# Four graph layers on one core: order of the prologue's loads and masks, and the feed-forward norms' engines

## The chip, the cores and the metric

The kernel runs on one core of a Trainium2 chip. A core has five engines that each work through their own list of instructions in order: TensorE (PE in the profile, with its weight loads as PEld), VectorE (DVE), ScalarE (ACT), GpSimd (POOL) and SyncE (SP), which here only issues loads and stores (DMAs). Engines wait for one another by semaphores. The metric is the device time of one execution in microseconds, taken as a median over runs; a separate execution is profiled, and all times of single instructions come from that one.

## The reference

For 16 batches of 1024 nodes with 256 features and one adjacency matrix, four layers follow one another, each with a residual:

```
h = relu(layernorm(x));  x = x + layer_L(h, adj)
layer 0, 1:  h = x @ W;  e = leaky_relu(h.a1[:, None] + h.a2[None, :])   # 1 head
             softmax over edges (adj != 0 in layer 0, adj > 0 in layer 1) @ h;  relu (0) or elu (1)
layer 2:     8 heads of dot-product attention, masked by adj > 0;  t
             x1 = layernorm(x + t) * ln1_g + ln1_b
             f  = relu(x1 @ w1 + b1) @ w2 + b2
             layernorm(x1 + f) * ln2_g + ln2_b
layer 3:     as layer 1 with 4 heads of 64, elu
```

In the inputs the biases are zero and the gains one, but the kernel computes with them as given.

## The kernel before

All lines are those of the profile. The function `fast_path` holds the whole work; `general_path` runs only if a check at the end fails, and did not run. The kernel writes out the order of instructions by hand: what the program emits first on an engine runs first there.

**Prologue (L314 to L400).** `load_x(0)` loads the first batch in one DMA on SP's queue (L317). `gat_weights` (L334) loads a layer's weights (L340) and its two attention vectors (L344), spread to all 128 partitions, on ACT's queue, and forms the products W.a1 and W.a2 on VectorE (L349), which become three more columns per head of the weights `wx`. Layer 0's come first. Then, for each of eight row blocks, the adjacency is loaded (L364), compared with zero in two ways (L367: `mask_nz` for layer 0, `mask_pos` for the others; the same instruction counts the degree), transposed by TensorE (L370, eight transposes) and copied by ScalarE into a byte mask (L371). Then come the loads of batches 1 and 2, layer 1's weights, the weights of layer 2 with gains and offsets (`spread`, L331) and layer 3's weights, whose eight vectors share three buffers with their products.

**Main loop.** The work of a layer and batch is a `Stage`. Its way in (`way_in`) is, for each of eight row blocks: statistics (`stats_of`: L501, L503 on VectorE, then the reciprocal root on GpSimd, L505 and L506), the normalized rows, transposes (L518, copied out at L519), the projection (L523), and in the layers 0, 1 and 3 the exponentials and scaled values (L563 to L572). Then weights and aggregation: in layers 0 and 1 `gat_front` spreads the source terms (L624, L629) and makes weights (L634), and `gat_back` multiplies (L647); in layer 2 `dot_front` makes scores (L811), exponentials (L817) and masks them (L822), and `dot_back` multiplies (L833); in layer 3 `pair_front` makes weights (L707) and `pair_back` multiplies (L727, L738).

Aggregation is cut into slots. After each slot `side_work` emits what is due of a queue: pieces put there by `later` or `chain` with a delay, and with a guess of their PE and DVE time, of which a slot takes at most 1.8 to 3.0 us each. `settle` empties the queue as far as needed when the next stage must be ready. Batches go in pairs: layers 0 and 1 of a pair, then layer 2 of both, then layer 3 mixed with layers 0 and 1 of the next pair.

**Feed-forward norms.** After the attention of half a batch, `feed_forward` takes four row blocks through `stats`, `norm`, `turn` (transposes into TensorE's layout and adds b2 to the rows on GpSimd, L898), two matrix products and a second norm (`finish`). `norm` calls `affine` (L511 to L513), which uses three engines in turn:

```
nc.scalar.activation(y, y, AF.Identity, scale=-1.0, bias=m)          # m - y
nc.vector.scalar_tensor_tensor(y, y, r, g, ALU.mult, ALU.mult)       # (m - y) r g
nc.gpsimd.tensor_tensor(y, b, y, ALU.subtract)                       # b - that
```

**Layer 3's elu** (`pair_out`): GpSimd takes one from x (L781) while ScalarE forms exp(y) (L785); VectorE then adds max(y, 0) (L788) and min(exp(y), 1) (L789).

Of the kernel before, what the change touches and what calls it, by code (L numbers as in the profile page):

```python
# [37 lines left out]
P = 128  # L38
# [13 lines left out]
def flat(a):  # L52
    return a.rearrange("f o -> (f o)")


def one_row(v):
    return v.rearrange("(o f) -> o f", o=1)
# [230 lines left out]
def fast_path(tc, bad, x, adj, l0_w, l0_a, l1_w, l1_a, w_qkv, ln1_g, ln1_b, ln2_g, ln2_b, w1, b1, w2, b2, l3_w, l3_a, out):  # L288
# [13 lines left out]
    with ctx:  # L302
# [12 lines left out]
        def load_x(b):  # L315
            xs[b] = state.tile([P, NT, C], F32, tag="x", name=f"x{b}", bufs=3)
            nc.sync.dma_start(out=xs[b], in_=x[b].rearrange("(t p) c -> p t c", p=P))  # L317
# [6 lines left out]
        ident_b = work.tile([P, P], BF16, tag="o", name="ident_b", bufs=2)  # L324
# [4 lines left out]
        def spread(v, name):  # L329
            t = const.tile([P, v.shape[0]], F32, name=name)  # L330
            nc.scalar.dma_start(out=t, in_=one_row(v).to_broadcast([P, v.shape[0]]))  # L331
            return t

        def gat_weights(w_heads, a1s, a2s, alpha, name):  # L334
# [4 lines left out]
            for h in range(heads):  # L339
                nc.scalar.dma_start(out=wx[:, :, h * hs : (h + 1) * hs], in_=rows(w_heads[h]))  # L340
            for h in range(heads):
                for a, uses in ((a1s[h], ((0, alpha - 1.0),)), (a2s[h], ((1, 1.0 - alpha), (2, alpha)))):
                    ab = work.tile([P, hs], F32, tag="xn", name="ab", bufs=3)
                    nc.scalar.dma_start(out=ab, in_=one_row(a).to_broadcast([P, hs]))  # L344
                    for part, factor in uses:
                        for k in range(KC):
                            col = C + part * heads + h
                            scr = work.tile([P, hs], F32, tag="xn", name="scr", bufs=3)
                            nc.vector.scalar_tensor_tensor(  # L349
                                scr, wx[:, k, h * hs : (h + 1) * hs], factor, ab, ALU.mult, ALU.mult,  # L350
                                accum_out=wx[:, k, col : col + 1],
                            )
            return wx

        wx0 = gat_weights([l0_w], [flat(l0_a[:C])], [flat(l0_a[C:])], ALPHA[0], "l0")
# [6 lines left out]
        for t in range(NT):  # L362
            edges = work.tile([P, N], I32, tag="p", name="edges", bufs=9)
            nc.sync.dma_start(out=edges, in_=adj[t * P : (t + 1) * P, :])  # L364
            for which, (op, mask) in enumerate(((ALU.not_equal, mask_nz), (ALU.is_gt, mask_pos))):
                m = work.tile([P, N], BF16, tag="p", name="m", bufs=9)
                nc.vector.tensor_scalar(m, edges, 0.0, 0.0, op, ALU.add, accum_out=degree[:, which, t : t + 1])  # L367
                tp = ps_mm.tile([P, NT, P], BF16, tag="mm", name="tp_mask")
                for j in range(NT):
                    nc.tensor.transpose(tp[:, j, :], m[:, j * P : (j + 1) * P], ident_b)  # L370
                nc.scalar.copy(mask[:, :, t * P : (t + 1) * P], tp)  # L371

        load_x(1)
        load_x(2)

        wx1 = gat_weights([l1_w], [flat(l1_a[:C])], [flat(l1_a[C:])], ALPHA[1], "l1")
        qkv_sb = const.tile([P, KC, 3 * C], F32, name="qkv_sb")
        nc.scalar.dma_start(out=qkv_sb, in_=rows(w_qkv))
        w1_sb = const.tile([P, KC, C], F32, name="w1_sb")
        nc.scalar.dma_start(out=w1_sb, in_=rows(w1))  # L380
        w2_sb = const.tile([P, KC, C], F32, name="w2_sb")
        nc.scalar.dma_start(out=w2_sb, in_=rows(w2))
        b1_sb = const.tile([P, KC, 1], F32, name="b1_sb")
        nc.scalar.dma_start(out=b1_sb, in_=b1.rearrange("(k p o) -> p k o", p=P, o=1))
        g1_sb, be1_sb = spread(ln1_g, "g1_sb"), spread(ln1_b, "be1_sb")
        g2_sb, be2_sb = spread(ln2_g, "g2_sb"), spread(ln2_b, "be2_sb")
        b2_sb = spread(b2, "b2_sb")
        wx3 = gat_weights(
            [l3_w[h] for h in range(H3)], [l3_a[h, :HS3] for h in range(H3)],
            [l3_a[h, HS3:] for h in range(H3)], ALPHA[3], "l3",  # L390
        )
        WX = {0: wx0, 1: wx1, 2: qkv_sb[:, :, 2 * C :], 3: wx3}
# [116 lines left out]
        def affine(y, m, r, g, b):  # L509

            nc.scalar.activation(y, y, AF.Identity, scale=-1.0, bias=m)  # L511
            nc.vector.scalar_tensor_tensor(y, y, r, g, ALU.mult, ALU.mult)  # L512
            nc.gpsimd.tensor_tensor(y, b, y, ALU.subtract)  # L513
# [237 lines left out]
        def pair_out(s, hp):  # L751
# [15 lines left out]
            for n in range(NH):  # L767
# [5 lines left out]
                def turn(n=n, y3=y3, xo=xo):  # L773
# [7 lines left out]
                    nc.gpsimd.tensor_scalar(xo, xo, -1.0, None, ALU.add)  # L781


                def power(ex=ex, y3=y3):
                    nc.scalar.activation(ex, y3, AF.Exp)  # L785

                def leave(n=n, ts=ts, ex=ex, y3=y3, xo=xo):
                    nc.vector.scalar_tensor_tensor(xo, y3, 0.0, xo, ALU.max, ALU.add)  # L788
                    nc.vector.scalar_tensor_tensor(xo, ex, 1.0, xo, ALU.min, ALU.add)  # L789
# [91 lines left out]
        def feed_forward(s, n):  # L881
            T_of = {"turned": 0}
            for i in range(TH):
# [10 lines left out]
                def turn(yt=yt, i=i):  # L894
# [3 lines left out]
                    nc.gpsimd.tensor_add(yt, yt, b2_sb)  # L898

                def turned(turn=turn):  # L900
# [6 lines left out]
                    (2.0, stats, 0.0, 0.6, None), (3.0, norm, 0.0, 0.5, None),  # L907
# [15 lines left out]
            def finish(t, i):  # L923
# [18 lines left out]
                chain((2.5, second, 0.9, 1.0, None), (3.0, norm, 0.0, 0.5, None))  # L942
# [58 lines left out]
        for t in range(NT):  # L1001
            way_in(by_key[0, 0], t, 1.0 * t)
        settle(by_key[0, 0])
        for s, piece in early:
            piece()

# [84 lines left out]
```

## Time and profile before

| | us |
|---|---|
| median of 3 runs | 4930.01 (4928.68 to 4932.11) |
| the profiled execution | 4923.55 |
| its span, first to last instruction | 4921.7 |
| mean granted TensorE clock | 0.980 |
| first layer norm starts | 78.31 |
| first aggregation on TensorE starts | 102.54 |
| one pair of batches, start to start | 601 |

The profile names a group by line, engine, operation and what it writes and reads; then come busy time, the mean of one in ns, and the idle time of the engine just before such instructions with what ended it. A stretch's row gives its length, the busy time of each engine and the granted TensorE clock. The clock is 1.00 for most of the run and drops to half for some us at a time; a stretch's number is the mean. A busy PE is not a PE at its peak.

### The profile page before, as it was taken

Reading aid. Unit: us, or ns where it says so; the run is one execution under the profiler, and the core shown is the slowest. Engines: PE = TensorE matmul, PEld = TensorE weight load, DVE = VectorE, ACT = ScalarE, POOL = GpSimd, SP = SyncE. Lnnn points to the kernel's source line nnn. Section 1 sums busy time; section 2 is a strip of 40 time slices with the busy share of each in tenths; the row PEclk is TensorE's granted clock in tenths of the full one; section 3 lists DMA queues with packets and bytes.
Section 4 is the critical chain, followed back from the end, with each engine's and each line's share of the span. In section 5 each row is a group of like instructions: output and inputs, shape, how many; then the busy total and the mean of one; then the engine's idle time right before and its main releaser. Section 6 shows DMA issues by size and latency. Waiting matters only on the chain.

```text
span 4921.7 us, 61508 instructions
## 1 busy us (share of the span) xinstructions
PE 4572.1 (93%) x22546; PEld 2264.1 (46%) x22546; DVE 3522.8 (72%) x5992; ACT 2219.7 (45%) x4017; POOL 1990.7 (40%) x2424
## 2 busy tenths in 40 slices
PE   4999899998999989999899998999999999999997
PEld 3843357433573335733357334562346623565232
DVE  4558876688756877578775788757877588775787
ACT  2356532564335642366323663236633466334651
POOL 1315642155422553225532356313653145531453
PEclk9999999999999999999999999999999999999999
DMA  2000010000100000000010000100010000100001
GB/s 89 1 1 1 18 35 18 1 1 18 35 18 1 1 18 35 18 1 18 1 46 7 1 18 9 44 1 1 18 34 19 1 1 18 35 9 1 1 18 36
DMA packets 50917, 79.13 MB, mean 16 GB/s; under 512 B 5680, under 2 KB 41136, under 8 KB 50608
## 3 DMA queue, kind: packets, MB, share of 16 engines
q1 hardware_dynamic: 45440, 71.58, 4.3%
q10 hardware_dynamic: 5168, 3.54, 0.3%
q8 instruction: 181, 2.97, 0.2%
q14 instruction: 128, 1.05, 0.1%
HBM read 58.07 MB, written 17.04 MB: 15 GB/s over the span
## 4 chain that ended last, share of the span: by engine, by line
PE 73%; DVE 10%; ACT 6%; POOL 6%; issue 3%; DVEq 0%; DMA 0%; ACTq 0%; POOLq 0%
PE pm L523 17%; PE av L647 17%; PE acc L833 12%; PE sc L811 10%; PE acc L727 8%; PE sums L738 4%; DVE p L707 3%; PE tp L518 3%; DVE pe L822 2%; POOL y L513 2%; ACT pe L817 2%; POOL rstd L506 2%; PE rp L624 1%; DVE y L512 1%; POOL rstd L505 1%
## 5 line engine op out<-in xcount | busy, mean ns | idle before, releaser
L822 DVE TENSOR_TENSOR pe<-pe,mask_pos 128x1024 f32<-128x1024 f32 x1024 | 1304.6, 1320 | 383.8 <-ACT pe L817 383.2
L817 ACT ACTIVATE pe<-sc 128x1024 f32<-128x1024 f32 x1024 | 991.8, 1021 | 448.0 <-PE sc L811 447.9
L833 PE MATMUL acc<-pe,v 128*33 128x512 f32 x4096 | 1010.4, 615 | 21.9 <-DVE pe L822 21.8
L505 POOL TENSOR_SCALAR rstd<-stats 128x1 f32<-128x1 f32 x768 | 398.2, 519 | 1421.8 <-DVE stats L503 1400.9
L647 PE MATMUL av<-v,p 128*128 128x257 f32 x4096 | 946.0, 380 | 0.8 <-DVE p L634 0.7
L647 PEld LDWEIGHTS av<-v,p 128*128 128x128 f32 x4096 | 756.3, 190 | 129.2 <-issue 28.8
L506 POOL TENSOR_TENSOR rstd<-rstd,minus_half 128x1 f32<-128x1 f32 x768 | 655.8, 854 | 64.0
L811 PE MATMUL sc<-qT,kT 32*128 32x512 f32 x4096 | 650.1, 654 | 16.9 <-ACT pe L817 16.9
L707 DVE SCALAR_TENSOR_TENSOR p<-r,e,mask_pos 128x1024 f32<-128x1024 f32 x512 | 654.8, 1324 | 13.8 <-PE sums L738 13.4
L833 PEld LDWEIGHTS acc<-pe,v 128*33 128x33 f32 x4096 | 198.4, 112 | 754.6 <-issue 422.3
L727 PE MATMUL acc<-p,v 128*64 128x512 f32 x2048 | 483.3, 614 | 3.1 <-ACT e L568 3.1
L523 PE MATMUL pm<-l_wx,hT 128*128 128x259 f32 (+1 forms) x1536 | 418.2, 403 | 27.6 <-ACT v L570 19.5
L864 POOL TENSOR_TENSOR y<-y,z 128x256 f32<-128x256 f32 x128 | 97.3, 768 | 794.8 <-DVE z L860 793.7
L523 PEld LDWEIGHTS pm<-l_wx,hT 128*128 128x128 f32 x1536 | 281.2, 194 | 173.4 <-issue 59.7
L519 ACT ACTIVATE hT<-tp 128x256 f32<-128x256 f32 x640 | 239.2, 384 | 265.2 <-PE tp L518 264.1
L811 PEld LDWEIGHTS sc<-qT,kT 32*128 32x128 f32 x4096 | 197.8, 185 | 315.6 <-ACT pe L817 203.4
L513 POOL TENSOR_TENSOR y<-be_sb,y 128x256 f32<-128x256 f32 x256 | 307.7, 1214 | 41.9 <-DVE y L512 41.6
L660 DVE RECIPROCAL inv<-av 128x1 f32<-128x1 f32 x256 | 42.8, 167 | 385.1 <-PE av L647 385.1
L518 PE MATMUL tp<-ident,xn 128*128 128x128 f32 x1024 | 206.3, 291 | 83.9 <-POOL rstd L505 44.1
L727 PEld LDWEIGHTS acc<-p,v 128*64 128x64 f32 x2048 | 138.5, 140 | 310.3 <-issue 246.1
L501 DVE BATCH_NORM_STATS2 st<-x 128x6 f32<-128x256 f32 x512 | 214.0, 418 | 91.3 <-POOL x L665 64.6
L665 POOL TENSOR_TENSOR x<-x,o 128x256 f32<-128x256 f32 x128 | 101.8, 796 | 387.7 <-ACT o L664 383.5
(98 smaller groups left out, 4872.7 us busy)
## 6 DMA issues: line engine op xcount, KB each, us to landing
r<-kept SPq DMA_DIRECT2D x64, 512.0 KB
x<-in_x_dram SPq DMA_DIRECT2D x16, 1024.0 KB
out_dram<-x SPq DMA_DIRECT2D x64, 256.0 KB
edges<-in_adj_dram SPq DMA_DIRECT2D x8, 512.0 KB
kept<-rows_sb SPq DMA_DIRECT2D x128, 2.0 KB
qkv_sb<-in_L_gnn_w_qkv_dram ACTq DMA_DIRECT2D x1, 768.0 KB
l_wx<-in_L_gnn_W_dram ACTq DMA_DIRECT2D x2, 256.0 KB
ab<-in_L_gnn_a_dram ACTq DMA_DIRECT2D x4, 128.0 KB
```

Source lines behind the costliest of these rows:

```text
L505: nc.gpsimd.tensor_scalar(r, stats[:, 1:2], EPS, None, ALU.add)
L506: nc.gpsimd.tensor_tensor(r, r, minus_half, ALU.pow)
L513: nc.gpsimd.tensor_tensor(y, b, y, ALU.subtract)
L518: nc.tensor.transpose(tp[:, k, :], src[:, k * P : (k + 1) * P], ident)
L523: nc.tensor.matmul(dst, lhsT=lhsT[:, k, :], rhs=rhs[:, k, :], start=(k == 0), stop=(k == KC - 1))
L647: nc.tensor.matmul(av[:, : s.hs + 1], lhsT=box[j // 2][:, j % 2, i * P : (i + 1) * P], rhs=s.v[:, j, h, :], start=(j == 0), stop=(j == NT ...
L707: nc.vector.scalar_tensor_tensor(p, s.r[hp][:, hh, :], s.e[:, j, col : col + 1], mask_pos[:, j, :], ALU.max, ALU.mult)
L727: both(lambda jj, n, hh, h, p: nc.tensor.matmul(s.acc[n][hh * hs : (hh + 1) * hs, :], lhsT=s.v[:, jj, h, :hs], rhs=p, start=(jj == 0), sto ...
L811: nc.tensor.matmul(sc[:, hh, :], lhsT=s.kT[r0 : r0 + D2, g, j * P : (j + 1) * P], rhs=s.qT[r0 : r0 + D2, g, cols], start=True, stop=True,)
L817: nc.scalar.activation(p, sc, AF.Exp, scale=SCALE2)
L822: nc.vector.tensor_tensor(box[pair], box[pair], m, ALU.mult)
L833: nc.tensor.matmul(s.acc[pair][hh * 64 : hh * 64 + D2 + 1, :], lhsT=s.v[:, j, h, :], rhs=box[pair][:, hh, :], start=(j == 0), stop=(j == N ...
```

## The change

- The first batch is loaded in halves. All loads but layer 0's weights and vectors go to SP's queue, in this order: batch 0, the eight blocks of adjacency, batch 1, the weights of layers 1 and 3, `qkv`, batch 2, the rest of layer 2's, and as the last two the second bias, once as a row and once as a column. The attention vectors of a layer come in one load of 256 KB. The adjacency stays in four large buffers.
- Layer 0's products come first, then its way in. Its mask is then made in two halves around the first weights. The other products (`fill1`, `fill3`), `fold_bias` and `mask_pos` become side work of the first slots.
- `affine` is two VectorE instructions. The second bias is added into the offset of the first norm, and w1 times it is taken from the first bias, so that L898 goes.
- Layer 3's elu: GpSimd's step goes; ScalarE forms relu(1 - exp(y)) and VectorE subtracts it.
- The guessed DVE time of `norm` is 1.0 in place of 0.5.

```diff
         def load_x(b):
-            nc.sync.dma_start(out=xs[b], in_=x[b].rearrange("(t p) c -> p t c", p=P))
+            for n in range(NH):
+                ts = slice(n * TH, (n + 1) * TH)
+                nc.sync.dma_start(out=xs[b][:, ts, :], in_=x[b, n * HALF : (n + 1) * HALF, :].rearrange("(t p) c -> p t c", p=P))
...
-        def gat_weights(w_heads, a1s, a2s, alpha, name):
+        def gat_weights(eng, w_heads, a, alpha, name):
...
-                    ab = work.tile([P, hs], F32, tag="xn", name="ab", bufs=3)
-                    nc.scalar.dma_start(out=ab, in_=one_row(a).to_broadcast([P, hs]))
+            ab = work.tile([P, 2 * C], F32, tag="p", name="ab", bufs=9)
+            eng.dma_start(out=ab, in_=one_row(a).to_broadcast([P, 2 * C]))
+            def fill(h):
...
+            return wx, [lambda h=h: fill(h) for h in range(heads)]
+        wx0, fill0 = gat_weights(nc.scalar, [l0_w], flat(l0_a), ALPHA[0], "l0")
+        edges = [state.tile([P, 2, N], I32, tag="big", name="edges", bufs=4) for _ in range(NT // 2)]
+        for t in range(NT):
+            nc.sync.dma_start(out=edges[t // 2][:, t % 2, :], in_=adj[t * P : (t + 1) * P, :])
+        load_x(1)
+        wx1, fill1 = gat_weights(nc.sync, [l1_w], flat(l1_a), ALPHA[1], "l1")
...
+        b2_row = work.tile([P, 2 * C], F32, tag="p", name="b2_row", bufs=9)
+        nc.sync.dma_start(out=b2_row[:, :C], in_=one_row(b2).to_broadcast([P, C]))
+        b2_col = const.tile([P, KC, 1], F32, name="b2_col")
+        nc.sync.dma_start(out=b2_col, in_=b2.rearrange("(k p o) -> p k o", p=P, o=1))
+
+        def fold_bias():
+            nc.vector.tensor_add(be1_sb, be1_sb, b2_row[:, :C])
+            for m in range(KC):
+                pm = ps_mm.tile([P, HALF], F32, tag="mm", name="pm_b")
+                for k in range(KC):
+                    nc.tensor.matmul(
+                        pm[:, :1], lhsT=w1_sb[:, k, m * P : (m + 1) * P], rhs=b2_col[:, k, :],
+                        start=(k == 0), stop=(k == KC - 1),
+                    )
+                nc.vector.tensor_tensor(b1_sb[:, m, :], b1_sb[:, m, :], pm[:, :1], ALU.subtract)
...
+        flags = state.tile([P, NT * C], F32, tag="y", name="flags").bitcast(BF16)
+        def mask_of(which, t):
+            op, mask = MASKS[which]
+            m = flags[:, (t % 4) * N : (t % 4 + 1) * N]
+            nc.vector.tensor_scalar(
+                m, edges[t // 2][:, t % 2, :], 0.0, 0.0, op, ALU.add, accum_out=degree[:, which, t : t + 1]
+            )
+            tp = ps_mm.tile([P, NT, P], BF16, tag="mm", name="tp_mask")
+            for j in range(NT):
+                nc.tensor.transpose(tp[:, j, :], m[:, j * P : (j + 1) * P], ident_b)
+            nc.scalar.copy(mask[:, :, t * P : (t + 1) * P], tp)
...
         def affine(y, m, r, g, b):
-            nc.scalar.activation(y, y, AF.Identity, scale=-1.0, bias=m)
-            nc.vector.scalar_tensor_tensor(y, y, r, g, ALU.mult, ALU.mult)
-            nc.gpsimd.tensor_tensor(y, b, y, ALU.subtract)
+            nc.vector.scalar_tensor_tensor(y, y, m, g, ALU.subtract, ALU.mult)
+            nc.vector.scalar_tensor_tensor(y, y, r, b, ALU.mult, ALU.add)
...
-                    nc.gpsimd.tensor_scalar(xo, xo, -1.0, None, ALU.add)
...
                 def power(ex=ex, y3=y3):
                     nc.scalar.activation(ex, y3, AF.Exp)
+                    nc.scalar.activation(ex, ex, AF.Relu, scale=-1.0, bias=1.0)
...
-                    nc.vector.scalar_tensor_tensor(xo, ex, 1.0, xo, ALU.min, ALU.add)
+                    nc.vector.tensor_tensor(xo, xo, ex, ALU.subtract)
...
-                    nc.gpsimd.tensor_add(yt, yt, b2_sb)
...
-                    (2.0, stats, 0.0, 0.6, None), (3.0, norm, 0.0, 0.5, None),
+                    (2.0, stats, 0.0, 0.6, None), (3.0, norm, 0.0, 1.0, None),
...
-                chain((2.5, second, 0.9, 1.0, None), (3.0, norm, 0.0, 0.5, None))
+                chain((2.5, second, 0.9, 1.0, None), (3.0, norm, 0.0, 1.0, None))
...
         for t in range(NT):
             way_in(by_key[0, 0], t, 1.0 * t)
+        for piece in fill0:
+            piece()
         settle(by_key[0, 0])
+        for t in range(TH):
+            mask_of(0, t)
         for s, piece in early:
             piece()
+        for t in range(TH, NT):
+            mask_of(0, t)
+        for i, piece in enumerate(fill1 + [fold_bias] + fill3):
+            later(0.5 + 1.0 * i, piece, 0.6, 1.3)
+        for t in range(NT):
+            later(20.0 + 3.0 * t, lambda t=t: mask_of(1, t), 0.6, 1.3)
```

## The prediction

> **What bounds the kernel now.** I read the page's engine rows first. TensorE (PE) is busy 93% of a span of 4921.7 us, and the first of forty slices is the one with a hole.
>
> ```profile
> PE 4572.1 (93%) x22546; PEld 2264.1 (46%) x22546; DVE 3522.8 (72%) x5992; ACT 2219.7 (45%) x4017; POOL 1990.7 (40%) x2424
> PE   4999899998999989999899998999999999999997
> ```
>
> So time is won only where PE stands idle or slow. There are two such places. The first is the prologue, seen in the table of stretches (length, busy time of PE, PEld, DVE, ACT, POOL, granted clock, DMA share, GB/s) and in the timeline of the first 105 us:
>
> ```profile
> 20.00:30.00 10.00, 9.12 (x72) 6.74 (x70) 10.00 (x18) 8.85 (x9) 0.00 (x0) 1.00 0.74 240
> 50.00:60.00 10.00, 0.00 (x0) 0.00 (x0) 1.05 (x12) 0.00 (x0) 0.00 (x0) 1.00 0.24 48
> 60.00:70.00 10.00, 0.00 (x0) 0.00 (x0) 1.43 (x16) 0.00 (x0) 0.00 (x0) 1.00 0.04 9
> ```
>
> ```profile
> 8.98 0.43 DVE L349 SCALAR_TENSOR_TENSOR scr<-l_wx,ab 128x256 f32<-128x256 f32 x1 [6.67 <-DMA ab<-in_L_gnn_a_dram]
> 13.97 1.22 DVE L367 TENSOR_SCALAR_CACHE_REDUCE m<-edges 128x1024 bf16<-128x1024 int32 x1
> 78.31 0.42 DVE L501 BATCH_NORM_STATS2 st<-x 128x6 f32<-128x256 f32 x1
> 100.63 0.15 DVE L613 TENSOR_REDUCE gat_seen<-e 128x1 f32<-128x8 f32 x1
> 102.54 10.53 PE L647 MATMUL av<-v,p 128*128 128x257 f32 x40 [0.74 <-DVE p L634]
> ```
>
> Both masks (L367) are done by 36 us. Then VectorE (DVE) works off the column products of layers 1 and 3 (L349), waiting for one small load after another, and only at 78.31 starts the first layer norm. PE has its first aggregation at 102.54. No data forces this: x was the first load.
>
> The second place recurs. The list of what PE waits for (us in total, times, longest), and the groups by cost (busy us, mean ns, idle before):
>
> ```profile
> PE tp L518 <- POOL y L513: 52.9, 53, 2.8
> PE tp L518 <- POOL rstd L505: 44.1, 1, 44.1
> PE tpo L856 <- ACT turned L847: 29.0, 32, 1.2
> PE tpo L856 <- DVE inv L858: 28.2, 16, 2.2
> ```
>
> ```profile
> L822 DVE TENSOR_TENSOR pe<-pe,mask_pos 128x1024 f32<-128x1024 f32 x1024 | 1304.6, 1320 | 383.8 <-ACT pe L817 383.2
> L513 POOL TENSOR_TENSOR y<-be_sb,y 128x256 f32<-128x256 f32 x256 | 307.7, 1214 | 41.9 <-DVE y L512 41.6
> L898 POOL TENSOR_TENSOR y<-y,b_sb 128x256 f32<-128x256 f32 x128 | 189.3, 1507 | 0.0
> L512 DVE SCALAR_TENSOR_TENSOR y<-y,rstd,g_sb 128x256 f32<-128x256 f32 x256 | 154.3, 644 | 11.3 <-ACT y L511 7.0 <-POOL rstd L506 3.2 <-POOL y L513 0.3
> L676 DVE SCALAR_TENSOR_TENSOR x<-o,x 128x256 f32<-128x256 f32 x128 | 54.5, 426 | 15.0 <-DVE x L675 1.4
> ```
>
> Outside the start, the GpSimd (POOL) step L513 of the feed-forward norm is PE's longest wait. Its row also shows contention: L513 and L898 take 1214 and 1507 ns, where the same shape takes 768 in L864; and L512 takes 644 where the same kind takes 426 in L676. The stalls cost clock as well. Stretches of one pair of batches (they repeat every 601 us), the last one around an L513 stall of 2.8 us:
>
> ```profile
> 1560.00:1650.00 90.00, 83.05 (x410) 27.37 (x406) 73.16 (x110) 58.50 (x85) 48.92 (x56) 0.96 0.00 1
> 1650.00:1760.00 110.00, 104.72 (x519) 35.24 (x519) 91.68 (x128) 69.17 (x98) 63.37 (x66) 0.98 0.06 20
> 1760.00:1800.00 40.00, 32.02 (x166) 11.28 (x162) 37.71 (x68) 13.73 (x31) 29.07 (x36) 0.95 0.00 1
> ...
> 1796.00:1811.00 15.00, 10.14 (x30) 4.23 (x30) 10.06 (x14) 3.58 (x10) 14.58 (x16) 0.66 0.01 2
> ```
>
> A clock of 0.66 over 15 us is 5.1 us of PE work lost behind the stall. DVE, at 37.7 of 40 us, is nearly full in the same place.
>
> **The change, term by term** (against the profiled execution, 4923.55 us with 1.85 around its span; it lies 6.5 under the median of 4930.0, so differences are carried over to the median).
>
> *Prologue, start.* The layer-0 products stay first on DVE, now behind one 256 KB load of both vectors. In the old run the 128 KB load was there at 8.98; from a load that shares the queues with x and the edges I estimate 11 us (9 to 14). Six products at 0.43 end at 13.6. The first statistics start there, 64.7 earlier than 78.31. What follows to gat_seen is the same instructions in the same order, so it ends at 100.8 - 64.7 = 36.1.
>
> *Prologue, layer-0 mask.* What was hidden before the norms now stands behind them. In DVE's order four mask rows come (L367, 1.14 apart: 4.6, to 40.7), then PE's transposes and ACT's copies of the last (1.0 and 1.0), the spread of the source (1.0) and its copy (0.6): 43.6. Then eight weights at 0.67 (L634 ran nine in 6.05): 49.0. Then four more mask rows: 53.6; PE must do these transposes and a second spread before its first aggregation: 55.5. In the old run PE started at 102.54, but went at DVE's pace for eight weights; I set its equivalent start at 103.5. So far 103.5 - 55.5 = 48.0 saved.
>
> *Moved load issues.* All but two loads now go through SP, 31 of them, each waiting for the one eight before. Some 10.9 MB at the 254 GB/s of the first 10 us is 43 us, so the last lands near 45. It matters: the fold of the second bias stands behind the first four aggregation matmuls on PE, and waits for the very last load; behind it stand all aggregations, and on DVE the weights of the next item. With 55.5 against 45 I take 0; if loads come later each us counts in full (bound +20, the last at 75, the pace of the old products).
>
> *mask_pos.* Eight rows move from idle PE into layer 0's side work. PE's 8 transposes per row cost 1.04 (L370: 16.6 us for 128); they directly follow their DVE instruction of 1.22, with no delay between, and five of the eight fall where layer 0 of the second batch is forced through with little aggregation beside it. Per row between 1.04 (all DVE time hidden) and 2.3 (all shown): I take 1.6, +13 (8 to 18). Other products: 6 at 0.43 and 24 at 0.22 now compete with the next eight weights; DVE has some 20 us of work where PE gives it 18.7: +4 (0 to 8).
>
> Prologue: -48 + 13 + 4 = **-31** (bounds -40 to -2).
>
> *Feed-forward norm.* ACT's L511 (113 us) and POOL's L513 go, DVE gets 256 more instructions; the 128 of L898 go for nothing, since the bias sits in the offset. On DVE: two instructions instead of one, each between 426 (L676) and 644 (L512). I take 480, nearer L676, because most of the POOL work that slowed L512 leaves: 512 x 0.48 - 154 = +92 us. In return L822 (1320 mean, 1180 in pairs that run without POOL: 2.36 for two at 426.14) should lose much of 1024 x 0.1, and L707 some. I book DVE's sum as even, 0 on the path (bounds -20; and +23 if nothing is won back: 8 affines fall into the full 40 us stretch, 8 x 0.644 = 5.2 against 2.3 us free, eight times).
>
> The L513 wait itself: 52.9 us of PE. The new y is ready after DVE alone, two slots before PE asks, but DVE is in order. I take two thirds as gone, -35 (0 to -53). The clock: stretches like the last one above lost 5.2, 3.4, 5.1 and 5.2 us in the first four pairs, 4.7 x 8 = 38; two thirds, -25 (0 to -44 with the smaller dips). Sum **-60**.
>
> The Trainium skill (TensorE: Matmul & The Clock Gate, What's actually happening) says that the array falls to half rate after an idle window of about 3.4 us; here waits of 2.8 and 1.3 us in sequence were enough, so I would follow the row, and by the rule alone the 25 would be 0. The same skill (SBUF — State Buffer, Who interferes with whom) speaks against the change: a DVE instruction with two SBUF inputs and a GpSimd instruction that reads SBUF exclude each other, and both new instructions have two. By it I would price them at L512's 644, DVE's sum would be +84 worse, and the total nearer -70.
>
> *Last elu.* POOL's L781 (1767 ns, 64) goes, ACT gets 64 at about 0.6 (38 us on an engine 45% busy), DVE's L789 becomes a plain subtraction. No PE wait is named after any of these: 0. Cover: ACT's slack before the two DVE instructions; without it 64 x 0.6 = +38, and -7 if L789 (801) falls to L788's 699.
>
> Sum: -31 - 60 = -91; 4930 - 91 = **4839**.
>
> **Rivals.**
> (a) Only the prologue counts: the L513 wait becomes a DVE wait of the same length, since DVE is 94% full where the stalls are worst. 4930 - 31 = 4899. For it: the 37.71 of 40. Against: DVE is only 81 to 83% full in the other two stretches.
> (b) The loads come late: SP's chain of eight with many small transfers at its end, the bias fold blocking PE. 4839 + 20 = 4859. For: small loads in the old run came 3 to 4 us apart; against: those were one at a time, here eight are under way.
> (c) Slower: DVE becomes the bound of layers 2 and 3. Its place is the norm cluster; its price 32 more instructions a pair at 0.644, 20.6 us, times 8 = 165 if all show. From 31 of the 165 on the path the prologue's gain is spent. With half, 4930 - 31 + 82 = 4981. Against: 37 us of DVE are free in the first two stretches of a pair, and POOL's slowing leaves.
> (d) All stalls and dips of L513 go and DVE's other waits shrink: 4930 - 40 - 53 - 44 = 4793.
>
> **How the numbers follow.** Forecast 0.62, (a) 0.17, (b) 0.08, (c) 0.06, (d) 0.07. The range 4795 to 4900 takes in (a) and (b) and nearly all of (d). About 0.2%, 10 us, is what this measurement tells from no change. Slower takes most of (c): 0.05; within 0.2% the rest of (c) and a bad (a): 0.04; faster 0.91.
>
> **What would show it.** Right: the first statistics near 14 us, the first aggregation near 56, the bias matmul without a wait; the period of a pair down from 601 to about 593; no PE wait on the norm above some 15 us; L822's mean near 1.25; more of the span at clock 1.0. Wrong: a first aggregation after 70, a DMA wait on PE, or "PE tp <- DVE y" in the place and size of L513's 52.9.

## The result, and the profile after

The changed kernel is slower by a third of a per cent: 4948.74 us median (4940.2 to 4951.57, 4 runs) against 4929.69 (4928.68 to 4932.11, 4 runs) of the kernel before; ratio 1.0035, 95% interval 1.0018 to 1.0052. Its profiled execution has a span of 4946.9 us (4921.7 before) and a mean granted clock of 0.971 (0.980).

Lines have moved: what was L822 (masked weights) is L849, L817 (exps) L844, L833 L860, L537 (xn) L564, L518 (transposes) L545, L501/L503 (statistics) L530/L532, L647 (aggregation) L674. L512 and L513 are now L539 and L540, both on VectorE. In runs that carry only a part of the change the same lines shift by a few.

The engines of the changed kernel, from the page (busy us, share, instructions):

```profile
PE 4582.5 (93%) x22554; PEld 2273.1 (46%) x22554; DVE 3522.8 (71%) x6251; ACT 2160.5 (44%) x3825; POOL 1369.8 (28%) x1976
```

VectorE's busy time is what it was to a tenth of a microsecond, 3522.8, with 259 instructions more. GpSimd lost 621 us. That VectorE's two sums agree to the tenth is chance. By busy time only TensorE is dearer, by 10.4 us; its waits and its clock have to be looked at.

The prologue, from the changed kernel's timeline (start, length, engine, line):

```profile
10.83 0.42 DVE L530 BATCH_NORM_STATS2 st<-x 128x6 f32<-128x256 f32 x1
...
33.22 0.15 DVE L640 TENSOR_REDUCE gat_seen<-e 128x1 f32<-128x8 f32 x1
...
53.76 1.91 PE L674 MATMUL av<-v,p 128*128 128x257 f32 x8
...
55.51 0.95 PE L396 MATMUL pm_b<-b_col,w_sb 128*128 128x1 f32 x8
```

The first statistics start at 10.83 (78.31 before), TensorE's first aggregation at 53.76 (102.54), and the bias matmul behind it waits for no load. The lead at this point is 48.8 us. But where layer 0 of batch 1 starts to aggregate, it is 131.0 against 153.5, 22.5 us, and from there a pair of batches takes 607.6 us where it took about 601.3: over the seven pairs that follow, the lead is spent and 25 us more.

What TensorE waits for in the changed kernel (us in total, times, longest):

```profile
PE tpo L883 <- ACT turned L874: 63.6, 48, 4.1
PE tp L545 <- ACT hT L546: 43.0, 60, 1.7
PE acc L860 <- DVE pe L849: 33.6, 32, 2.2
PE tp L545 <- ACT xn L564: 32.5, 8, 12.2
PE pm L550 <- ACT hT L546: 29.4, 33, 4.5
PE sc L838 <- ACT pe L844: 20.2, 8, 2.5
```

The wait on the norm's last step, 52.9 us before, is gone; in its place on VectorE ("tp <- DVE y L539") stand 2.8 us. But TensorE now waits for ScalarE: for turned copies 63.6 us (29.0 before), for hT copies ahead of transposes 43.0 (6.4) and ahead of projections 29.4 (5.5). The last two in the kernel before:

```profile
PE tp L518 <- ACT hT L519: 6.4, 19, 0.4
...
PE pm L523 <- ACT hT L519: 5.5, 19, 0.7
```

Clock went too: what the clock took is at most (1 - clock) x span (all of it only if TensorE has work throughout), 143 us against 98 before, to within some 5 us.

The groups that the prediction priced (busy us, mean ns, idle before):

```profile
L849 DVE TENSOR_TENSOR pe<-pe,mask_pos 128x1024 f32<-128x1024 f32 x1024 | 1226.6, 1244 | 399.1 <-ACT pe L844 399.1
...
L540 DVE SCALAR_TENSOR_TENSOR y<-y,rstd,be_sb 128x256 f32<-128x256 f32 x256 | 142.0, 555 | 27.5 <-DVE y L539 0.9
...
L539 DVE SCALAR_TENSOR_TENSOR y<-y,stats,g_sb 128x256 f32<-128x256 f32 x256 | 123.0, 480 | 0.0
```

The masked weights got 78 us back (1304.6 before), the norm took 265 instead of 154.

### The profile page after: what moved, and what is told of

The parts are those of the page before. It is cut to its first block, busy times and chain, and to the rows that moved or that the text cites. A ratio compares the mean times of both kernels' runs of the same rounds, so it can differ in the third digit from the quotient of the medians.

```text
span 4946.9 us, 61169 instructions
## 1 busy us (share of the span) xinstructions
PE 4582.5 (93%) x22554; PEld 2273.1 (46%) x22554; DVE 3522.8 (71%) x6251; ACT 2160.5 (44%) x3825; POOL 1369.8 (28%) x1976
## 4 chain that ended last, share of the span: by engine, by line
PE 68%; DVE 16%; ACT 6%; issue 2%; POOL 0%; DVEq 0%; ACTq 0%; POOLq 0%
PE pm L550 16%; PE av L674 14%; PE acc L860 13%; PE sc L838 9%; PE acc L754 7%; DVE pe L849 5%; PE sums L765 4%; DVE p L734 4%; PE tp L545 2%; DVE y L540 2%; ACT pe L844 1%; DVE y L539 1%; DVE st L530 1%; PE rp L651 1%; ACT turned L874 1%
## 5 line engine op out<-in xcount | busy, mean ns | idle before, releaser
L849 DVE TENSOR_TENSOR pe<-pe,mask_pos 128x1024 f32<-128x1024 f32 x1024 | 1226.6, 1244 | 399.1 <-ACT pe L844 399.1
L844 ACT ACTIVATE pe<-sc 128x1024 f32<-128x1024 f32 x1024 | 992.3, 1021 | 524.1 <-PE sc L838 524.1
L860 PE MATMUL acc<-pe,v 128*33 128x512 f32 x4096 | 1004.1, 609 | 34.3 <-DVE pe L849 33.6
L674 PE MATMUL av<-v,p 128*128 128x257 f32 x4096 | 945.8, 381 | 0.0
L674 PEld LDWEIGHTS av<-v,p 128*128 128x128 f32 x4096 | 757.4, 190 | 126.6 <-issue 27.4
L534 POOL TENSOR_SCALAR rstd<-stats 128x1 f32<-128x1 f32 x768 | 380.1, 495 | 1527.6 <-DVE stats L532 1513.0
L734 DVE SCALAR_TENSOR_TENSOR p<-r,e,mask_pos 128x1024 f32<-128x1024 f32 x512 | 643.7, 1303 | 47.0 <-PE sums L765 47.0
L535 POOL TENSOR_TENSOR rstd<-rstd,minus_half 128x1 f32<-128x1 f32 x768 | 629.8, 820 | 64.0
L860 PEld LDWEIGHTS acc<-pe,v 128*33 128x33 f32 x4096 | 194.5, 111 | 778.7 <-issue 394.7
L550 PE MATMUL pm<-l_wx,hT 128*128 128x259 f32 (+1 forms) x1536 | 431.5, 412 | 58.0 <-ACT hT L546 29.4
L545 PE MATMUL tp<-ident,xn 128*128 128x128 f32 x1024 | 202.6, 288 | 97.0 <-ACT xn L564 32.5
L590 ACT ACTIVATE e<-pm,rstd 128x3 f32<-128x3 f32 (+1 forms) x256 | 67.9, 265 | 475.9 <-PE pm L550 474.4
L765 PE MATMUL sums<-p,e 128*32 128x512 f32 x2048 | 263.0, 634 | 0.0
L530 DVE BATCH_NORM_STATS2 st<-x 128x6 f32<-128x256 f32 x512 | 212.8, 416 | 51.1 <-POOL x L692 48.6
```

What stands on the lines that cost most here:

```text
L534: nc.gpsimd.tensor_scalar(r, stats[:, 1:2], EPS, None, ALU.add)
L535: nc.gpsimd.tensor_tensor(r, r, minus_half, ALU.pow)
L545: nc.tensor.transpose(tp[:, k, :], src[:, k * P : (k + 1) * P], ident)
L550: nc.tensor.matmul(dst, lhsT=lhsT[:, k, :], rhs=rhs[:, k, :], start=(k == 0), stop=(k == KC - 1))
L674: nc.tensor.matmul(av[:, : s.hs + 1], lhsT=box[j // 2][:, j % 2, i * P : (i + 1) * P], rhs=s.v[:, j, h, :], start=(j == 0), stop=(j == NT ...
L734: nc.vector.scalar_tensor_tensor(p, s.r[hp][:, hh, :], s.e[:, j, col : col + 1], mask_pos[:, j, :], ALU.max, ALU.mult)
```

## The experiments

Each ratio is to runs of the kernel before on the same chip; the medians of the kernel before lie between 4921.1 and 4932.1 us from chip to chip, 0.2%, so ratios are compared, not times.

### Which part of the change loses

**The prologue alone**: the old norm, elu and cost guess put back by the edits shown below, and the second bias added by GpSimd as before.

> The changed prologue alone, with the norm, the second bias, the elu and the guesses of before (the check tile at the very end shares a buffer, for space). If the loss sits in the recurring part and comes from norm, guess or elu: the pair of batches takes 601 us as before, and the time is that of before less the 22 us by which the changed kernel still leads when the second batch's layer 0 begins to aggregate, near 4908. If the prologue's side work shifts the queue so that every pair gets longer: a pair of 605 to 608 us and 4930 or more.

4909.49 us, ratio 0.9965 (0.9951 to 0.9979), as expected of a loss that sits in norm, guess or elu.

**All but the norm**: the new kernel with the old `affine` and guess.

```diff
-            nc.vector.scalar_tensor_tensor(y, y, m, g, ALU.subtract, ALU.mult)
-            nc.vector.scalar_tensor_tensor(y, y, r, b, ALU.mult, ALU.add)
+            nc.scalar.activation(y, y, AF.Identity, scale=-1.0, bias=m)
+            nc.vector.scalar_tensor_tensor(y, y, r, g, ALU.mult, ALU.mult)
+            nc.gpsimd.tensor_tensor(y, b, y, ALU.subtract)
```

> The changed kernel with the three-engine norm and its guess of 0.5; the bias stays folded, the elu new. Theory norm (the 256 additional VectorE instructions make VectorE late; ScalarE waits in order for its statistics, and TensorE for ScalarE): the pair falls back to 601 us or under, since GpSimd is freed of the bias addition, 4895 to 4908. Theory elu (ScalarE's additional relu): stays above 4935.

4925.76 us, 0.9998 (0.9989 to 1.0007), between what the two theories allowed. So the norm with its guess loses about 0.4%, and something between this run and the one before it loses about 0.3%.

**The guess**: the planner's cost of both norms back from 1.0 to 0.5, all else new (the call of the first norm alike).

```diff
...
-                chain((2.5, second, 0.9, 1.0, None), (3.0, norm, 0.0, 1.0, None))
+                chain((2.5, second, 0.9, 1.0, None), (3.0, norm, 0.0, 0.5, None))
```

> The changed kernel with the guess of the norm's VectorE time back at 0.5, so that up to four norms are emitted in a slot in place of two. Theory guess (the emission order that follows from 1.0 bunches statistics and holds TensorE up): 4908 or less, pair 601. Theory norm (VectorE's work itself): 4940 to 4955, pair 607 to 609.

4958.39 us, 1.0068 (1.0055 to 1.0082). With the old guess it is worse, a little beyond what theory norm allowed; the guess isn't the cause.

**The old elu**, all else new: GpSimd's step back, ScalarE's new one out.

```diff
+                    nc.gpsimd.tensor_scalar(xo, xo, -1.0, None, ALU.add)
...
-                    nc.scalar.activation(ex, ex, AF.Relu, scale=-1.0, bias=1.0)
...
-                    nc.vector.tensor_tensor(xo, xo, ex, ALU.subtract)
+                    nc.vector.scalar_tensor_tensor(xo, ex, 1.0, xo, ALU.min, ALU.add)
```

> The changed kernel with the elu of before (GpSimd subtracts one, VectorE takes the minimum). Theory elu: 4915 to 4930. Theories norm and guess: 4945 to 4955, as the changed kernel or a few us above, since GpSimd's 64 long instructions are back and slow VectorE.

4947.18 us, 1.0043 (1.003 to 1.0057): no gain from undoing the elu, beside the new norm and its guess of 1.0.

### Two attempts to take ScalarE's wait away

In the changed kernel ScalarE stands 102.3 us waiting for VectorE's statistics ahead of xn (L564), 41 times, with exps and copies queued behind:

```profile
ACT xn L564 <- DVE stats L532: 102.3, 41, 4.1
```

If that is the link, taking xn off ScalarE, or asking for it later, should give the time back, provided that neither brings a new wait.

**xn on GpSimd**, in layers 0 and 3:

```diff
-                    nc.scalar.activation(xn, xs[s.b][:, t, :], AF.Identity, scale=-1.0, bias=box["m"])
+                    nc.gpsimd.tensor_scalar(xn, xs[s.b][:, t, :], box["m"], None, ALU.subtract)
...
```

The sign of xn turns round by this, so the copies behind the transposes lose their factor of -1.

> The changed kernel whole, but the centred copies xn of layers 0 and 3 (mean subtracted, 128x256) are made by GpSimd instead of ScalarE, which in the changed kernel waits 102.3 us in all, 41 times, for VectorE's statistics (20.8 us in the run with the prologue alone), with the exps, turned copies and hT copies queued behind it. Theory A, that the norm on VectorE makes the statistics late and ScalarE's in-order queue passes that on to TensorE: at least the 22 us between the changed kernel and the run with the old norm come back, ratio to the kernel before 0.999 or lower (it was 1.0035), TensorE's waits for turned copies back from 63.6 us to about 29 and its waits for hT copies before transposes from 43 to under 15. Rival B, that VectorE's 256 added instructions are themselves what the end waits for: the waits turn to VectorE's masked weights (33.6 us now) and the ratio stays at 1.002 to 1.005. Rival C, that GpSimd becomes the late engine in ScalarE's place (its instructions of this size, 64 a pair, at 1 us or more each, and the reciprocal roots queued behind): 1.005 or higher.

5079.0 us, 1.0316 (1.0302 to 1.033). TensorE's list of waits:

```profile
PE tp L545 <- POOL xn L564: 231.5, 115, 16.2
PE acc L860 <- DVE pe L849: 41.9, 40, 2.2
PE tpo L883 <- ACT turned L874: 38.2, 48, 1.2
```

The wait for turned copies did fall from 63.6, but GpSimd was late with xn itself, 231.5 us. Rival C was right, and more so than it said. (There are 32 such instructions in a pair and 256 in all, half of what this expectation, and that of the prologue with the same edit, say.)

**xn later**, in the way in:

```diff
-                (3.0, norm, 0.0, (0.0, 0.4, 0.7, 0.0)[s.layer], rings["xn"].free),
+                (6.0 if s.layer == 3 or (s.layer == 0 and s.b >= 2) else 3.0, norm, 0.0, (0.0, 0.4, 0.7, 0.0)[s.layer], rings["xn"].free),
```

> The changed kernel whole, but in layer 3 and, from batch 2 on, in layer 0 the step that makes xn is ordered 6 units of TensorE's work behind its statistics instead of 3; nothing else is moved by hand, and no instruction is added or taken away. Theory A: ScalarE's wait for the statistics falls from 102.3 to under 40 us and half or more of the lost 22 us come back, ratio 0.999 to 1.001. Rival B (VectorE's volume is the bound): ratio stays at 1.002 to 1.005. Rival D: the later step makes the transposes and the projections of the next layer late instead, since they keep their distance behind xn: ratio above 1.005.

4997.05 us, 1.0151 (1.0137 to 1.0165). The statistics were waited for half as long, as the list for ScalarE shows:

```profile
ACT xn L564 <- DVE stats L532: 54.2, 50, 4.7
```

and yet it is slower, as rival D had it: transposes and projections came late in turn. Both runs put a new wait in the place of the old one, so they don't refute that ScalarE's queue passes VectorE's lateness on; they show that this link can't be taken out so.

**The prologue alone, with xn on GpSimd** by the same edit.

> The changed prologue alone, with old norm, old bias addition and old elu, and xn of layers 0 and 3 on GpSimd. ScalarE is freed of some 512 instructions there, but its wait for statistics is only 20.8 us in this kernel. Theory A says that little is to be had: 0.994 to 0.997 (0.9965 without). If GpSimd's lateness matters (it has 41% of the span to do in the kernel before and would get over 50%): above 0.998.

5245.45 us, 1.0659 (1.0644 to 1.0673). A GpSimd with 40% of the span busy is no free place.

**Prologue and fold** of the second bias, with old norm, elu and guess, run beside these.

> The changed prologue and the second bias folded into the offset, old three-engine norm, old elu: the run with the prologue alone (0.9965) plus the fold. It splits the 16 us between that run and the one with fold and new elu (0.9998). If the fold costs them: 0.999 to 1.0005. If the new elu does: 0.996 to 0.997. If neither, and the period of a pair only settles at another multiple of the clock's window: anything between, with no new wait over 10 us in TensorE's list.

4895.36 us, 0.9955 (0.9941 to 0.9968). The fold costs nothing that these intervals show, so the 0.0043 up to 0.9998 are the new elu's. This run is the base of the next ones.

### One norm at a time, and VectorE's time by itself

On this base each engine's instructions keep their order, but for the norm's own; TensorE's are the same 22554 in the same order.

**Both norms on VectorE.**

> The run with prologue and fold (0.9955), with both feed-forward norms on VectorE and nothing else; every engine's instructions stay in the same order but for the norm's own. The cleanest price of the norm. Theory A (the two VectorE instructions of a norm stand in stretches of layer 2 where VectorE runs without a gap, ahead of the masked weights and of the next layer's statistics, and ScalarE's and TensorE's queues hold still behind them): 1.000 to 1.006, 22 to 50 us more. Rival E (the loss comes from the change of the planner's cost 0.5 to 1.0, or from the new elu, and the norm is even): 0.994 to 0.997.

4951.67 us, 1.004 (1.0026 to 1.0053).

**The first norm alone** (`affine_v` is the new form):

```diff
-                    affine(yt, box["m"], box["r"], g1_sb, be1_sb)
+                    affine_v(yt, box["m"], box["r"], g1_sb, be1_sb)
```

> As the run with both norms on VectorE, but only the norm ahead of the feed-forward block (128 of the 256); its result is waited for by TensorE's transposes, 51.5 us in the run with prologue and fold. Theory A, with the harm in the second norm, which stands ahead of the next layer's statistics: that wait goes and little is lost, 0.992 to 0.997. Theory F (each of VectorE's added instructions costs the same, wherever it is): half of what both norms cost, 0.998 to 1.001.

4874.8 us, 0.9879 (0.9864 to 0.9895): the fastest kernel of the study, below what either theory said. Two rows of TensorE's list in the base:

```profile
PE tp L546 <- POOL y L541: 51.5, 52, 2.8
...
PE tp L546 <- ACT v L598: 23.3, 39, 2.4
```

With the first norm on VectorE the wait for its last step (the first row) is gone, but other waits grew, above all the one for scaled values:

```profile
PE tp L550 <- ACT v L602: 50.4, 39, 4.8
```

So which wait the gain comes from isn't shown. (The two profiled executions, on different chips, lie only 13 us apart.)

**The second norm alone**: the same edit at the call with `g2_sb`.

> As the run with both norms on VectorE, but only the norm behind the feed-forward block, which is followed by the residual addition on GpSimd and the statistics of the next layer. Theory A, harm in the second norm: 0.999 to 1.005. Theory F: half of what both cost, 0.998 to 1.001. If it is faster than the run with prologue and fold (0.9955), the second norm is a gain and the first one the loss.

4997.51 us, 1.0135 (1.0119 to 1.015). From the base, -0.0076 and +0.0180, together +0.0104; both at once measured +0.0085. The same two instructions gain in one place and lose in the other, and the loss is larger than theory A said (0.999 to 1.005).

**VectorE's time alone**: the old norm stays on its three engines, and behind each second norm VectorE reads a tile for nothing.

```diff
                     affine(yt, box["m"], box["r"], g2_sb, be2_sb)
+                    nc.vector.bn_stats(small.tile([P, 6], F32, tag="spare", name="spare", bufs=3), xt)
```

> The run with prologue and fold, old norm, and behind each second norm one more VectorE instruction whose result nobody reads (the statistics of a 128x256 tile, about 0.40 us, 128 of them; a norm of two VectorE instructions takes 0.32 us more of VectorE than the old one). ScalarE's and GpSimd's parts of the norm stay. It prices VectorE's time alone, at the place in question. If VectorE's time is what is lost: 0.998 to 1.003. If VectorE has the room and the loss comes from what else the new norm changes (GpSimd's buffer of time between the norm and the statistics gone, all four engines in step): 0.995 to 0.9965.

4992.89 us, 1.0124 (1.0109 to 1.014), 0.0169 above the base, again more than expected: about 83 us for 53.3 us of VectorE.

```profile
L966 DVE BATCH_NORM_STATS2 spare<-x 128x6 f32<-128x256 f32 x128 | 53.3, 416 | 0.0
```

Nothing else was added. The one thing that could wait for it, GpSimd's residual addition, which writes the tile that it reads, starts at least 0.6 us behind it each time, straight after GpSimd's own step before. So here VectorE's time is on the path, with interest.

Where the time goes can be told for every instruction of TensorE, since they come in the same order. How much later they are than in the base, by stretches of a pair (us from its first aggregation, mean of pairs 2 to 7):

| stretch | second norms there (base) | second norm on VectorE | extra VectorE instruction |
|---|---|---|---|
| 0 to 350 | | -0.5 | +0.1 |
| 350 to 400 | 1st four | +4.3 | +4.3 |
| 400 to 475 | 2nd four | +5.1 | +3.7 |
| 475 to 575 | 3rd four | +0.1 | +0.4 |
| 575 to the end, near 601 | 4th four | +3.4 | +2.7 |
| whole pair | | +12.4 | +11.3 |

Both runs lose at the same three of the second norm's four places, and nearly nothing elsewhere. The place can be seen. In the base, near the end of layer 2's first batch of a pair (timeline; in brackets the idle time before and what ended it):

```profile
2180.27 0.88 DVE L540 SCALAR_TENSOR_TENSOR y<-y,rstd,g_sb 128x256 f32<-128x256 f32 x2
...
2185.21 1.81 DVE L540 SCALAR_TENSOR_TENSOR y<-y,rstd,g_sb 128x256 f32<-128x256 f32 x2
2185.55 1.14 PE L839 MATMUL sc<-qT,kT 32*128 32x512 f32 x8
...
2187.39 0.18 DVE L532 BATCH_NORM_AGGREGATE stats<-st 128x2 f32<-128x6 f32 x1
...
2187.67 1.04 ACT L565 ACTIVATE xn<-x,stats 128x256 f32<-128x256 f32 x2 [2.15 <-POOL y L892]
...
2188.61 1.92 ACT L845 ACTIVATE pe<-sc 128x1024 f32<-128x1024 f32 x2
2189.67 2.04 PE L839 MATMUL sc<-qT,kT 32*128 32x512 f32 x8 [1.13 <-ACT pe L845]
```

The same instructions in the run with the second norm on VectorE:

```profile
2216.00 0.48 DVE L544 SCALAR_TENSOR_TENSOR y<-y,stats,g_sb 128x256 f32<-128x256 f32 x1
...
2217.57 0.77 DVE L545 SCALAR_TENSOR_TENSOR y<-y,rstd,be_sb 128x256 f32<-128x256 f32 x1
...
2219.41 3.17 DVE L854 TENSOR_TENSOR pe<-pe,mask_pos 128x1024 f32<-128x1024 f32 x2
...
2221.29 1.14 PE L843 MATMUL sc<-qT,kT 32*128 32x512 f32 x8
...
2222.50 0.47 DVE L544 SCALAR_TENSOR_TENSOR y<-y,stats,g_sb 128x256 f32<-128x256 f32 x1
...
2225.20 0.18 DVE L532 BATCH_NORM_AGGREGATE stats<-st 128x2 f32<-128x6 f32 x1
...
2225.48 1.04 ACT L569 ACTIVATE xn<-x,stats 128x256 f32<-128x256 f32 x2 [4.23 <-DVE stats L532]
...
2226.42 1.92 ACT L849 ACTIVATE pe<-sc 128x1024 f32<-128x1024 f32 x2
2227.48 2.14 PE L843 MATMUL sc<-qT,kT 32*128 32x512 f32 x6 [3.20 <-ACT pe L849]
```

Two norms take VectorE 0.88 us in the base (1.81 the second time, beside a busy GpSimd), and 2.34 in the other from first to last (2216.00 to 2218.34). All of it stands ahead of two masked weights, two more norms and the statistics of layer 3. ScalarE can't pass the xn that waits for them; the exps come behind it, and TensorE's next scores wait for a place that the exps free: 3.20 us instead of 1.13. From one group of scores to the next it is 6.19 us instead of 4.12.

Over the whole run, in the base:

```profile
ACT xn L565 <- POOL x L966: 35.0, 17, 6.8
ACT xn L565 <- POOL y L541: 30.5, 33, 2.0
ACT xn L565 <- POOL y L892: 17.4, 8, 2.3
ACT xn L565 <- DVE stats L532: 16.9, 11, 4.3
```

```profile
PE pm L551 <- ACT v L598: 25.5, 23, 1.5
...
PE sc L839 <- ACT pe L845: 17.3, 16, 1.4
```

and with the second norm on VectorE:

```profile
ACT xn L569 <- DVE stats L532: 140.2, 53, 14.7
```

```profile
PE sc L843 <- ACT pe L849: 47.9, 16, 3.2
PE pm L555 <- ACT v L602: 38.5, 23, 3.4
```

ScalarE always stood about 100 us ahead of xn, by the profile mostly for GpSimd (L541 and L892 write y, which xn doesn't read, so their names may be wrong). These rows went and VectorE's grew past them, to 140. TensorE lost 44 us in the two rows shown. The clock, 0.967 against 0.978 over these spans, took up to another 57; TensorE's busy time for the same matmuls grew by 46 (4616.6 against 4570.6). The span grew by 100. That VectorE's lateness reaches TensorE through ScalarE's queue is read from these timelines and lists; no run took this link out by itself.

### Does it hold the other way, and the elu

**The changed kernel with the second norm alone undone** (guess 0.5).

> The changed kernel with its second norm alone put back to three engines (and the planner's cost of a norm back at 0.5): prologue, fold, new elu and the first norm on VectorE stay. If the second norm is the whole of what the change loses: the 0.9879 of the run with the first norm plus what the new elu cost in the pairs of runs before (0.0028 to 0.0043), so 0.990 to 0.9925, faster than both kernels. If the new elu costs nothing beside the first norm: 0.987 to 0.989. If the parts do not add up, and the first norm's gain hung on the old elu: 0.996 or higher.

4881.35 us, 0.9921 (0.9907 to 0.9934): without the second norm the change beats the kernel before by 0.8%. Beside the run with the guess alone undone (1.0068) the second norm costs 0.0147, more than the whole of the loss. Against the run with the first norm and the old elu (0.9879) it is 0.0042 slower, the price of the new elu again.

**The second norm off VectorE**, beside the first one on it:

```diff
+            nc.scalar.activation(y, y, AF.Identity, scale=-1.0, bias=m)
+            nc.scalar.activation(y, y, AF.Copy, scale=r)
+            nc.gpsimd.tensor_tensor(y, y, g, ALU.mult)
+            nc.gpsimd.tensor_tensor(y, b, y, ALU.subtract)
```

> The run with the first norm on VectorE (0.9879), and the second norm with no VectorE instruction after its statistics: two steps on ScalarE, two on GpSimd; 128 VectorE instructions of some 0.64 us (82 us in all) gone from the place where 51 us more cost 83 us. If VectorE's time there is what sets the pace, and ScalarE and GpSimd have the room: 0.970 to 0.982. If ScalarE's added 128 instructions, in the same queue as the exps, or GpSimd's, ahead of the residual addition and the next statistics, set it instead: 0.990 to 1.010, with the waits for statistics on GpSimd.

4965.57 us, 1.0092 (1.0076 to 1.0107). Its waits, ScalarE's and TensorE's:

```profile
ACT xn L575 <- POOL y L550: 70.4, 36, 3.3
```

```profile
PE sc L849 <- ACT pe L855: 43.8, 32, 1.9
```

The scores wait for the exps about as long as with the norm on VectorE (47.9), now behind GpSimd's step and ScalarE's own. Whether VectorE's time taken away without adding to another engine would gain, stays open.

**One more ScalarE instruction in the old elu**, on the base: a relu over exp(y), whose values are positive already. (The expectation says 32 steps; it ran 64 times, 40.4 us.)

```diff
                     nc.scalar.activation(ex, y3, AF.Exp)
+                    nc.scalar.activation(ex, ex, AF.Relu)
```

> The run with prologue and fold (0.9955), old elu, and one more ScalarE instruction in each of the last elu's 32 power steps (a relu over values that are positive already): what the new elu adds to ScalarE, without what it takes from GpSimd and VectorE. If ScalarE's time there is what the new elu costs: 0.998 to 1.000, as with the whole new elu (0.9998). If it is not: 0.995 to 0.9965.

4916.73 us, 0.9993 (0.9984 to 1.0002), 0.0038 above the base; the whole new elu cost 0.0043. TensorE's wait for scaled values rose as it did there:

```profile
PE pm L551 <- ACT v L598: 33.5, 24, 2.6
```

So it is ScalarE's 40 us that the new elu pays with. What it takes from GpSimd brings nothing that shows.

## Why the prediction was wrong

*Prologue start: right, in part by luck.* 48 us at the first aggregation were predicted, 48.8 came. The load of the two vectors was earlier than taken (first statistics 10.83, not 13.6), the mask and weights of layer 0 took a little longer. (The steps listed for the mask add up to 44.3, not 43.6.) Loads: nothing waited for the last one, as booked.

*mask_pos and the products: mis-sized.* 13 + 4 were booked, about 26 came (48.8 down to 22.5); no run tells the one from the other. So the prologue is worth about 22 us rather than 31; alone it measured 0.35%, with the fold 0.45%, which is 17 and 22 us.

*VectorE's sum even: right. "0 on the path": the step that failed.* The norm took 111 us more where 92 were booked (480 and 555 ns in place of 480 each), the masked weights and others gave it back, and VectorE ended at 3522.8 as before. But the two don't lie in the same place. At three of its four places in a pair the second norm stands where VectorE, ScalarE and TensorE follow one another without slack, and what the masked weights win elsewhere doesn't come back there. The extra VectorE instruction priced these places: 53 us of work, 83 us of time; the second norm alone cost 0.0180, some 89 us.

The outer bound of 8 x 2.9 us looked at another place. The stretch from 1760 to 1800, with VectorE full for 37.7 of 40 us, holds four norms and not eight, all of them first norms (L512 at 1793.4 to 1795.2), and in the mean TensorE lost next to nothing there in the two runs of the table (475 to 575). Two of the three places that cost lie in the stretches that were read as 81 to 83% full: VectorE is busy 23.3 of the 25 us from 1600 in the kernel before, and 20.3 of the 22 from 1678. A mean over 90 or 110 us hid these. (The 37 us called free in these two are 35.2.) And the bound counted VectorE's busy time, not the wait of ScalarE's queue behind it.

*The wait on L513: it went, and the worth came out for one norm, though not shown to be by this mechanism.* It went wholly, not by two thirds. With the first norm alone the kernel is 0.0076 faster than its base, some 37 us where 35 were booked for the wait, but TensorE's list gives most of the wait back under other names (transposes behind ScalarE's v 50.4 us against 23.3, behind rows_sb 19.6 against 10.7, behind hT copies 15.8 against 6.1). So the agreement may be luck. With the second norm there was nothing to win of this kind: behind it no transposes wait for y, but the residual and the next statistics.

*The clock: wrong in sign.* 25 us were to come back; up to 45 more were lost, since new stalls took the place of the old. The Trainium skill (TensorE: Matmul & The Clock Gate, What's actually happening) lets the array fall to half rate after an idle window of about 3.4 us. In the run with the second norm on VectorE two of the waits that grew are 3.2 and 3.4 us at their longest, and the clock still took up to 57 us more. Behind its first 160 us TensorE is idle for over 3.4 us only twice, both times in the last 100 us, yet 62 half-rate stretches lie there, against 41 in the base. By the page's rule alone next to nothing of that was to be expected; this case's traces don't agree with it.

*The last elu: booked at 0 with a bound of +38; it is about +21 beside the old norms (0.0043).* Its bound held. Beside both new norms undoing it brought nothing with the guess at 1.0, and 0.0028 with the guess at 0.5. The cover named was ScalarE's slack; the run with one more ScalarE instruction shows that it takes up about half: 40 us of work cost 0.0038, 19 us.

Of the rivals, (c) had the mechanism and nearly the place (the norms, but not which of them), and let VectorE's instructions alone set the price; (a), a wait of the same size on VectorE in L513's place, wasn't seen: the wait showed up on ScalarE. The parts, in ratio: prologue -0.0035, fold -0.0010, first norm -0.0076, second +0.0161 beside it, elu +0.0028 beside both, guess about -0.0033.

## What to carry to other kernels

An instruction that moves to a fuller engine is to be priced at each place where it runs, by what stands behind it in that engine's queue and who waits for that, not by the engine's sum: the same edit was worth -0.8% at one call and +1.8% at the other. To price a place, add one instruction there whose result nobody reads, and measure; it took one run to tell what the busy times could not. A busy share over a long stretch hides the places in it that are full. Where a change mixes places, try them one at a time before giving it up: the changed kernel with one call undone is 0.8% faster than before, and with the old elu as well 1.2%.

## What the runs showed of the hardware

The time of a pair of batches comes in steps. Half-rate stretches of the granted clock last 3.413 us or a multiple in the traces. The period from one pair's layer 0 to the next (pairs 2 to 8), over all 17 profiled executions, lies within 0.5 us of a whole number of 3.413 us in 88 of 102 cases; about 30 would by chance, and a step of 3.40 or 3.42 catches 4. It is 604.1 to 604.4 in all six of the prologue alone (177 steps), 607.6 in five of six of the changed kernel (178), 597.2 to 597.6 and 600.5 to 601.1 in the run with the second norm undone (175 and 176), 624.4 to 624.7 in five of six with xn on GpSimd (183). One step in each of eight pairs is 27 us, 0.55%. From 241 us on the prologue alone has the same instructions in the same order on every engine as the kernel before, and its profiled period is still 604.2 against about 601 (at 4922.9 us this execution was the slowest of its five). So a stall of a microsecond can cost nothing or a whole step, which is the likeliest reason why single parts of this change don't add up to better than 0.2%; no run was made to show it by itself.

GpSimd at work beside VectorE goes with slower VectorE instructions, by a size seen here: masked weights of 128x1024 took 1320 ns in the mean in the kernel before, 1308 with the prologue alone, 1285 without GpSimd's bias addition, and 1244 in the changed kernel, without its part of the norm and the elu as well. GpSimd's busy share alone doesn't set it: in the run with the second norm off VectorE GpSimd is busy 35% of the span, against 28% in the changed kernel, and the mean is 1244 too.
